# Fetching fewer neighbour rows in a graph kernel: the last tile of each group skips its fetch, and some places are fetched for part of the partitions

## Chip, cores and metric

The kernel runs on one core of a Trainium2 chip, as one launch. The metric is the device time of that launch in microseconds; the median of three runs stands for a kernel. Engines are named as in the profile: PE (matrix products and transposes), DVE (vector), ACT (scalar), POOL (GpSimd), SP (sync).

## The reference, cut to what matters

Sixteen graphs of 1024 nodes have 64 features per node, and a sparse weighted adjacency matrix each. Two residual layers follow each other.

```python
# layer 0
h = maximum(layernorm(x), 0);  x = x + (adj / clip(rowsum(adj), 1)) @ h
# layer 1
h = maximum(layernorm(x), 0)
nb  = neighbours of a node, itself left out
m   = number of neighbours
if m > 10: drop every ceil(m/2)-th neighbour, symmetrically
agg = 0.25*q25 + 0.5*q50 + 0.25*q75     # per channel, interpolated quantiles
                                        # of h over the node and its kept neighbours
x = x + (relu((h + agg) @ W1 + b1) @ W2 + b2) * mask
```

The quantiles need each node's neighbour rows, sorted channel by channel. Most nodes have few neighbours: the adjacency is built so that low node numbers have many and high ones hardly any.

## The kernel before, in words

**Layer 0.** For each graph, pairs of 128-row blocks of the adjacency matrix are loaded by DMAs that ACT issues, turned by PE, copied to SBUF by ACT and multiplied with h. Beside it DVE lists the neighbours of each row (`signs`, `listing`), and `endings` gives each node a place in an order by falling neighbour count. POOL then scatters the node rows to a table `srt` in that order (eight indirect DMAs for one graph), and SP writes the normalized rows to `tab`. A last row of `tab` for each graph holds 1e30 in the channels and -1 behind them: the row of a neighbour that is not there.

**Groups.** Four graphs make a group, and there are four groups. In a group, the sorted nodes are cut into 32 tiles of 128 partitions. Each tile holds 32 successive ranks of each of the four graphs, and a quarter of it (32 partitions) holds 8 successive ranks of each. `CAPS` (line 36) gives the number of neighbours that a tile provides for: 15 for tile 1, then 10, 8, 7, 7, 6 and so on to 1 for tiles 27 to 31. Tile 0, with the nodes of very many neighbours, is handled separately as four long lists. Tiles of one cap form a `Job` (line 875), ten jobs in each group.

**A job.** `Job.run` takes a buffer A (`places`, four of them in turn) with a slot for the node and one for each neighbour. POOL fills one slot of one tile with one indirect DMA of 128 rows (`gather`, line 854): 124 of these for each group. A neighbour that is not there has the index of the 1e30 row. Then `sort` has DVE mark dropped neighbours and run a sorting network with min and max, `weigh` multiplies the sorted places with the weights of the quantiles, and `layers` sums them on PE and runs the two small products. DVE adds the residual to y, and POOL scatters y to the output, one indirect DMA for each tile. A flag (`checked`, line 1397) compares the neighbour counts with the caps; if a count is above its cap, a slow dense path runs in place of these results.

**Order.** DVE and POOL run in the order in which the program writes their instructions. That order is made by `Plan` (line 246), a list scheduler with a clock for each engine and a fixed cost for each operation: an indirect DMA costs 1.27 us on POOL, whatever its width (line 322), a copy on ACT 0.06 us and 0.86 ns for each element. Among the streams ready first, rank decides. The work on ACT, PE and SP is put into order by the tile framework's own scheduler. All engines take their queues strictly in order. The groups 0 to 2 are begun while layer 0 still runs for later graphs; group 3 and the long lists (`lplaces`) come after layer 0.

Of the kernel before, what the change touches and what calls it, by code (L numbers as in the profile page):

```python
# [9 lines left out]
F32 = mybir.dt.float32  # L10
# [8 lines left out]
P = 128  # L19
# [4 lines left out]
HUGE = 1.0e30  # L24
# [11 lines left out]
CAPS = (  # L36
    [0, 15, 10, 8, 7, 7, 6] + [5] * 4 + [4] * 4 + [3] * 6 + [2] * 6 + [1] * 5
)
CAPS2 = [CAPS[1]] + CAPS[2::2]
LONG = (88, 28, 21, 18)  # L40
MAIN = 38
LENT = 20
# [203 lines left out]
class Plan:  # L246
# [25 lines left out]
    def room(self, name, bufs):  # L272

        tiles = self.slots.get(name, ())
        if len(tiles) < bufs:
            return 0.0
        old = tiles[-bufs]
        return INF if self.users[old] else max(self.used.get(old, 0.0), self.ready.get(old, 0.0))

    def at(self, *tiles):  # L280
        return max(self.ready.get(t.tensor.name, INF) for t in tiles)
# [72 lines left out]
def kernel(  # L354
# [27 lines left out]
    with tc.manual_schedule(engines={mybir.EngineType.DVE, mybir.EngineType.Pool}):  # L382
        list_path(tc, x, adj, nodemask, w1, b1, w2, b2, out, go)
# [7 lines left out]
def list_path(ctx, tc, x, adj, nodemask, w1, b1, w2, b2, out, go):  # L391
    nc = tc.nc
    B, N, C = x.shape
# [8 lines left out]
    W = C + 2  # L402
# [4 lines left out]
    RW = R0 + REC  # L407
    NTAU = len(CAPS)
    HP = P // 2
    NF = NG + NG + len(LONG)  # L410

    consts = ctx.enter_context(tc.tile_pool(name="consts", bufs=1))
# [51 lines left out]
    caps4 = consts.tile([P, NTAU], F32, name="caps4")  # L464
    for t, cap in enumerate(CAPS):
        nc.vector.memset(caps4[:, t:t + 1], float(cap if t else N))
    caps2 = consts.tile([P, NTAU // 2], F32, name="caps2")
    for t, cap in enumerate(CAPS2):
        nc.vector.memset(caps2[:, t:t + 1], float(cap))
    nc.vector.memset(caps2[HP:, 0:1], float(N))  # L470

# [33 lines left out]
    turn = consts.tile([P, 1], F32, name="turn")  # L505
    ovf = consts.tile([P, NF], F32, name="ovf")
    nc.vector.memset(ovf, 0.0)
# [5 lines left out]
    tabs = [dram.tile([n * TS, W], F32, name=f"tab{g}") for g, n in enumerate(GROUPS)]  # L513
    whole = dram.tile([B * TS, W], F32, name="whole")
    srt = [dram.tile([GROUPS[g] * N, RW], F32, name=f"srt{g}") for g in range(NG)]
    none = consts.tile([B, W], F32, name="none")
    nc.vector.memset(none[:, :C], HUGE)
    nc.vector.memset(none[:, C:], -1.0)
    for tab, n in zip(tabs, GROUPS):
        nc.sync.dma_start(tab.rearrange("(b t) w -> b t w", t=TS)[:, N, :], none[:n])  # L520
    adj_rows = adj.rearrange("b i j -> (b i) j")
# [4 lines left out]
    plan = Plan(nc)  # L526
    plan.parts.update(tab.tensor.name for tab in tabs)
    nc = plan.nc
# [325 lines left out]
    def gather(dst, src, idx):  # L854
        nc.gpsimd.indirect_dma_start(
            out=dst, out_offset=None, in_=src,
            in_offset=bass.IndirectOffsetOnAxis(ap=idx, axis=0),
        )

    def scatter(dst, src, idx, others):  # L860
        if plan.last is others:
            nc.gpsimd.memset(turn, 0.0)
        ins = nc.gpsimd.indirect_dma_start(
            out=dst, out_offset=bass.IndirectOffsetOnAxis(ap=idx, axis=0),
            in_=src, in_offset=None,
        )

        for other in others:
            tc.declare_no_dep(ins.ins, other, reason="rows of their own")
        others.append(ins.ins)  # L870
        plan.last = others
# [3 lines left out]
    class Job:  # L875
# [1 line left out]


        def __init__(self, pool, n, T, keys, idx, node, mask, nodes_i, table, S, g, name="places",
                     bufs=4, rank=0, half=False, begin=0.0, shared=None, first=0):  # L880
            self.__dict__.update(locals())
            self.short = pool is gat
            self.tag = "" if self.short else "l0" if name == "lplaces0" else "l"
            self.block = BLOCK if self.tag == "l0" else n
            self.bufs1 = 1 if self.tag == "l0" else 2

        def run(self):
            n, T, pool, short = self.n, self.T, self.pool, self.short

            since = []  # L890
            own = () if short else (lambda rank: self.rank,)
            pace = lambda: since[0] + 1.3 * len(since) if not short else 0.0
            yield "POOL", lambda: max(
                self.begin, at(self.idx), room(self.name, self.bufs),
                room("S", 4) if short and not (self.shared and "S" in self.shared) else 0.0,
            ), *own
            A = self.A = new(pool, [P, n, T, W], F32, self.name, self.bufs, users=1)
            lent = LENT if self.tag == "l0" else 0
            order = [*range(lent), *range(n - 1 - MAIN, n - 1)] if lent else range(n - 1)
            progress["ahead"] += T * len(order)  # L900
            parts = self.parts() if self.block < n else None
            if short:
                mine, share = self.S, self.shared
                if share is None:
                    share = {"users": 1, "rows": mine}
                if "S" not in share:
                    S = share["S"] = new(
                        pool, [P, mine_of(share), C], F32, "S", 4, users=share["users"]
                    )
                    nc.sync.dma_start(S, share["rows"][:, :, :C])  # L910
                self.share = share
                self.S = share["S"][:, self.first:self.first + T, :]
            for t in range(T):
                for k in order:
                    if t or k:
                        yield "POOL", pace, *own
                    since.append(since[0] if since else plan.clock["POOL"])
                    plan.own = plan.clock["POOL"]
                    gather(A[:, k + 1, t, :], self.table, self.idx[:, t, k:k + 1])
                    plan.own = None  # L920
                    progress["ahead"] -= 1
                    if k == lent - 1:
                        plan.add(self.moves(parts), self.rank)
                    elif parts and k >= lent and ((k + 2) % self.block == 0 or k == n - 2):
                        plan.add(parts(-(-(k + 2) // self.block) - 1), self.rank)
            if parts:
                yield "DVE", lambda: self.landed if self.left == 0 else INF, self.soon
                yield from self.merge()
                return
            yield "DVE", lambda: max(  # L930
                at(A, self.S) + SLACK,
                *(room(self.tag + name, self.bufs1) for name in ("gone", "wu")),
            ), self.soon
            yield from self.sort()
# [226 lines left out]
        def layers(self, terms, sources):  # L1161
# [63 lines left out]
            for t in range(T):  # L1225
                yield "POOL", lambda: at(y) + LATE
                top = HP if self.half and t == 0 else P
                scatter(out_rows, y[:top, t, :], self.nodes_i[:top, t:t + 1], scatters)
# [70 lines left out]
    def group(g, kept=grp, name=""):  # L1299

        assert GROUPS[g] == 4
        caps, begin, NTAU = CAPS, 1, len(CAPS)
# [76 lines left out]
        dropped = at(table)  # L1379
# [45 lines left out]
        shared = {"users": len(few), "rows": tiles[:, front, :R0]}  # L1425
        for i, ts in enumerate(classes):
            n, T = caps[ts[0]] + 1, len(ts)
            sl = slice(ts[0], ts[-1] + 1)
            job = Job(
                gat, n, T, keys[:, sl, :n - 1], idx[:, sl, :], node[:, sl], mask[:, sl],  # L1430
                nodes_i[:, sl], table, tiles[:, sl, :R0], g,
                half=0 in ts, begin=dropped,
                **(dict(shared=shared, first=ts[0] - few[0][0]) if ts in few else {}),
            )
            plan.add(job.run(), 100 * g + i)
        progress["groups"] = g + 1

    def long_lists(pool):
# [14 lines left out]
        for e, (by, last) in enumerate(((5, 1), (7, 0))):  # L1453
# [4 lines left out]
            )  # L1458
        own_rows = new(pool, [P, len(LONG), RW], F32, "lS", 1)
        for g in range(NG):  # L1460
            lo, num = FIRST[g] * LSUB, GROUPS[g] * LSUB
            nc.sync.dma_start(
                own_rows[lo:lo + num, :, :],
                srt[g][:len(LONG) * num, :].rearrange("(l r) w -> r l w", l=len(LONG)),
            )
        for l in LORDER:
            K = LONG[l]
            n = K + 1
# [110 lines left out]
    for g in range(NG - 1):  # L1579
        plan.add(group(g), -2000)  # L1580
# [9 lines left out]
    with tc.tile_pool(name="long", bufs=1) as pool:  # L1590

        plan.add(group(NG - 1, pool, "last_"), -2000)
        plan.add(long_lists(pool), -1500)
        plan.run()
    nc = tc.nc
# [291 lines left out]
```

## Time and profile before

| | us |
|---|---|
| median of three runs (1734.42 to 1737.37) | 1736.29 |
| the profiled execution | 1737.01 |
| its span | 1735.1 |
| busy: DVE | 1200.8 |
| busy: POOL | 946.9 |
| busy: PE | 781.4 |
| busy: ACT | 557.5 |

The span runs from the first to the last instruction of the profiled execution. A helper records every operation, so nearly all rows carry line 240 (`Timed`); rows are told apart by the tiles that they write and read. On POOL, a row of an indirect DMA is the time on the engine, not the transfer.

### The profile page before, as it was taken

How to read it: one execution, taken by the hardware profiler on the slowest of the kernel's cores; microseconds unless marked ns; L12 is line 12 of the kernel's file. 1: busy time of each engine (PE TensorE's matmuls, PEld its weight loads, DVE VectorE, ACT ScalarE, POOL GpSimd, SP SyncE). 2: the span in 40 equal slices, each digit the busy share in tenths (PEclk: the TensorE clock that was granted, in tenths of full speed). 3: DMA queues.
4: the chain of work that ended last, by engine and by line, in shares of the span. 5: the costliest groups of instructions: out<-in, count | busy, mean ns of one | idle time of the engine just before them, and what ended most of it. 6: DMA issues, size and time to landing. Idle time of an engine off the chain costs nothing. (4 is left out here: it accounts for less than half of the span.)

```text
span 1735.1 us, 14258 instructions
## 1 busy us (share of the span) xinstructions
PE 781.4 (45%) x3203; PEld 483.9 (28%) x3203; DVE 1200.8 (69%) x4061; ACT 557.5 (32%) x1603; POOL 946.9 (55%) x1117
## 2 busy tenths in 40 slices
PE   5877634522686426627644644310200303116576
PEld 3434312321353223314422322200100202114355
DVE  7787954684587356829854655587699536899496
ACT  7766724351373333626533432200000001000011
POOL 0222372575545646554557256576687774658463
PEclk9888866765888666768766866555555556556667
DMA  4454732341154231424523311321211111012000
GB/s 167 149 178 139 205 90 65 108 122 23 45 148 156 64 99 41 140 46 136 150 51 87 93 30 43 72 60 38 50 26 24 25 24 24 19 20 41 15 22 14
DMA packets 133833, 132.30 MB, mean 76 GB/s; under 512 B 99444, under 2 KB 102132, under 8 KB 133620
## 3 DMA queue, kind: packets, MB, share of 16 engines
q10 hardware_dynamic: 34048, 71.31, 12.4%
q0 software_dynamic: 31520, 40.19, 10.6%
q1 hardware_dynamic: 68172, 19.82, 5.3%
q8 instruction: 27, 0.44, 0.1%
q14 instruction: 66, 0.54, 0.1%
HBM read 111.76 MB, written 23.61 MB: 78 GB/s over the span
## 5 line engine op out<-in xcount | busy, mean ns | idle before, releaser
L240 POOL DMA_INDIRECT places<-tab,idx x372 | 367.6, 988 | 121.6 <-issue 110.1
L240 PE MATMUL pt<-ident,prod 128*128 128x128 f32 (+1 forms) x736 | 152.5, 365 | 357.6 <-DVE prod L240 245.8
L240 POOL DMA_INDIRECT srt<-row,to x128 | 131.8, 1030 | 287.1 <-ACT row L240 268.1
L240 PE MATMUL ps_small<-att,h 128*65 128x512 f32 x512 | 266.8, 666 | 33.7 <-issue 19.3
L240 PE MATMUL pt<-ident,at 128*128 128x128 f32 x1024 | 191.6, 339 | 182.3 <-ACT att L240 104.7
L240 PEld LDWEIGHTS pt<-ident,prod 128*128 128x128 f32 (+1 forms) x736 | 123.4, 247 | 388.9 <-issue 211.9
L240 PEld LDWEIGHTS pt<-ident,at 128*128 128x128 f32 x1024 | 149.7, 175 | 239.9 <-ACT att L240 126.1
L240 ACT COPY att<-pt 128x512 f32<-128x512 f32 x256 | 143.3, 582 | 169.9 <-remote 98.3
L240 DVE MAX8 rec<-sg 128x8 f16<-128x256 f16 x512 | 180.1, 414 | 14.3 <-remote 6.4
L240 ACT COPY ot<-pt 128x128 f32<-128x128 f32 (+3 forms) x56 | 22.4, 400 | 476.7 <-remote 194.6
L240 POOL DMA_INDIRECT out_dram<-y,nodes_i x93 | 97.0, 1043 | 121.7 <-DVE y L240 81.4
L240 POOL DMA_INDIRECT places<-tab,last_idx x124 | 132.8, 1071 | 52.0 <-issue 37.1
L240 POOL DMA_INDIRECT lplaces<-whole,lidx x125 | 138.5, 1108 | 38.1 <-issue 37.2
L240 ACT ACTIVATE sg<-at 128x1024 f16<-128x1024 f32 x128 | 134.6, 1053 | 52.4 <-DVE rec L240 15.7
L240 PEld LDWEIGHTS ps_small<-att,h 128*65 128x65 f32 x512 | 77.2, 157 | 165.0 <-issue 144.4
L240 PE MATMUL ps_small<-ot,w_sb 128*128 128x128 f32 (+3 forms) x112 | 55.9, 591 | 127.8 <-ACT ot L240 80.9
L240 DVE TENSOR_TENSOR sg<-sg,keyed 128x1024 f16<-128x1024 f16 x128 | 87.3, 682 | 18.0 <-ACT sg L240 14.7
L240 DVE TENSOR_TENSOR places<-places,other 128x128 f32<-128x128 f32 (+6 forms) x160 | 56.4, 355 | 25.9 <-remote 12.4
L240 ACT ACTIVATE wu<-wu 128x39 f32<-128x39 f32 (+9 forms) x40 | 9.4, 234 | 191.8 <-DVE wu L240 166.2
L240 PE MATMUL ps_small<-w_sb,hid 128*128 128x64 f32 x256 | 53.2, 350 | 29.3 <-issue 21.6
L240 ACT ACTIVATE hid<-ps_small,b_sb 128x128 f32<-128x128 f32 (+2 forms) x56 | 28.1, 502 | 111.7 <-remote 72.9
L240 PEld LDWEIGHTS ps_small<-ot,w_sb 128*128 128x128 f32 (+1 forms) x112 | 23.2, 254 | 141.7 <-ACT ot L240 87.8
(289 smaller groups left out, 1621.3 us busy)
## 6 DMA issues: line engine op xcount, KB each, us to landing
at<-in_adj_dram ACTq DMA_DIRECT2D x64, 1024.0 KB
places<-tab,idx POOLq DMA_INDIRECT x372
whole<-tab SPq DMA_DIRECT2D x4, 1057.0 KB
tab<-row SPq DMA_DIRECT2D x16, 264.0 KB
xt<-in_x_dram ACTq DMA_DIRECT2D x16, 256.0 KB
S<-srt SPq DMA_DIRECT2D x12, 192.0 KB
y<-srt SPq DMA_DIRECT2D x12, 192.0 KB
srt<-row,to POOLq DMA_INDIRECT x128
```

Source lines behind the costliest of these rows:

```text
L240: ins = getattr(self._engine, op)(*args, **kwargs)
```

## The change

A table `QUARTERS` gives nine of the tiles a cap for each quarter. In each group tile 31 then gets no fetch at all, and eight places (three of tile 1 and one each of tiles 2, 5, 10, 20 and 26) are fetched for 32, 64 or 96 partitions only. The partitions that are left out get the row of a missing neighbour by ScalarE copies from a constant tile `void`, 32 partitions by 66 elements each. They are written in `run` ahead of the job's fetches. The comparison with the caps in `checked` uses the quarters' caps.

```diff
+QUARTERS = {
+    1: (15, 13, 12, 12), 2: (10, 10, 10, 9), 5: (7, 7, 6, 6), 10: (5, 5, 4, 4), 14: (4, 4, 4, 4),
+    20: (3, 3, 2, 2), 26: (2, 2, 1, 1), 30: (1, 1, 1, 1), 31: (0, 0, 0, 0)}
+def quarters(t):
+    return QUARTERS.get(t, (CAPS[t],) * 4)
...
+    for t in QUARTERS:
+        for q, cap in enumerate(quarters(t)):
+            nc.vector.memset(caps4[q * QUART:(q + 1) * QUART, t:t + 1], float(cap))
...
-    none = consts.tile([B, W], F32, name="none")
-    nc.vector.memset(none[:, :C], HUGE)
-    nc.vector.memset(none[:, C:], -1.0)
+    void = consts.tile([P, W], F32, name="void")
+    nc.vector.memset(void[:, :C], HUGE)
+    nc.vector.memset(void[:, C:], -1.0)
+    none = void[:B, :]
...
+            if short:
+                for t in range(T):
+                    for k in order:
+                        top = QUART * sum(cap > k for cap in quarters(self.tiles[t]))
+                        for low in range(top, P, QUART):
+                            nc.scalar.copy(
+                                A[low:low + QUART, k + 1, t, :], void[low:low + QUART, :]
+                            )
             for t in range(T):
                 for k in order:
...
-                    plan.own = plan.clock["POOL"]
-                    gather(A[:, k + 1, t, :], self.table, self.idx[:, t, k:k + 1])
-                    plan.own = None
+                    top = P
+                    if short:
+                        top = QUART * sum(cap > k for cap in quarters(self.tiles[t]))
+                    if top:
+                        plan.own = plan.clock["POOL"]
+                        gather(A[:top, k + 1, t, :], self.table, self.idx[:top, t, k:k + 1])
+                        plan.own = None
```

For each group this makes 123 fetches of 124, eight of them narrower (two of 32 partitions, five of 64, one of 96), and 21 copies on ACT. Over the kernel, that is 492 fetches in place of 496, 32 of them narrower, and 84 copies.

More of the change, by code (lines that the diff above doesn't have):

```diff
@@ L409, in list_path @@
     HP = P // 2
+    QUART = P // 4
     NF = NG + NG + len(LONG)
@@ L879, in __init__ @@
         def __init__(self, pool, n, T, keys, idx, node, mask, nodes_i, table, S, g, name="places",
-                     bufs=4, rank=0, half=False, begin=0.0, shared=None, first=0):
+                     bufs=4, rank=0, half=False, begin=0.0, shared=None, first=0,
+                     tiles_of=None):
             self.__dict__.update(locals())
             self.short = pool is gat
+            self.tiles = tiles_of
             self.tag = "" if self.short else "l0" if name == "lplaces0" else "l"
@@ L1431, in group @@
                 nodes_i[:, sl], table, tiles[:, sl, :R0], g,
-                half=0 in ts, begin=dropped,
+                half=0 in ts, tiles_of=ts, begin=dropped,
                 **(dict(shared=shared, first=ts[0] - few[0][0]) if ts in few else {}),
```

## The prediction

> **What bounds the kernel now.** I read the busy times and their rows by slice first, then the waits of POOL, the stretches of the span, and last the order of time at the end.
>
> ```profile
> PE 781.4 (45%) x3203; PEld 483.9 (28%) x3203; DVE 1200.8 (69%) x4061; ACT 557.5 (32%) x1603; POOL 946.9 (55%) x1117
> ...
> DVE  7787954684587356829854655587699536899496
> ACT  7766724351373333626533432200000001000011
> POOL 0222372575545646554557256576687774658463
> ...
> L240 POOL DMA_INDIRECT places<-tab,idx x372 | 367.6, 988 | 121.6 <-issue 110.1
> ```
>
> No engine is full. A fetch costs POOL 988 ns plus 0.30 us to the next one, so 1.25 to 1.29 us, and 0.7 busy on POOL is really about 0.9 occupied. The kernel has two stages. In the first (to about 1115 us, where the last node rows are scattered) layer 0 runs with the jobs of groups 0 to 2 between it. Here POOL waits for the others, as its waits of the first 1000 us show (total, times, longest):
>
> ```profile
> POOL srt L240 <- ACT row L240: 247.2, 25, 61.0
> POOL places L240 <- issue: 86.6, 284, 0.3
> POOL out_dram L240 <- DVE y L240: 71.5, 7, 13.7
> ```
>
> 247.2 us of waiting for finished node rows: a POOL that is done earlier only waits longer there. What holds this stage up are chains between ACT, PE and DVE, with DVE standing still up to 24 us at a time:
>
> ```profile
> 767.50 0.32 DVE L240 TENSOR_SCALAR ln_v<-ln_v 128x8 f32<-128x8 f32 x1 [23.98 <-remote]
> ```
>
> The second stage has the rest of group 2, the long lists and group 3. By stretches of 100 us (busy PE, PEld, DVE, ACT, POOL):
>
> ```profile
> 1300.00:1400.00 100.00, 16.48 (x56) 10.93 (x56) 76.37 (x234) 3.92 (x10) 78.05 (x73) 0.53 0.14 24
> 1400.00:1500.00 100.00, 16.19 (x82) 12.71 (x82) 64.03 (x196) 6.90 (x19) 60.77 (x73) 0.55 0.11 23
> 1500.00:1600.00 100.00, 39.25 (x167) 30.96 (x167) 92.19 (x279) 6.36 (x22) 67.20 (x65) 0.59 0.16 29
> ```
>
> Up to 1400 POOL feeds without a break (78 busy and 73 gaps of 0.3 make 100). From 1500 on DVE is the full one. POOL's order of time at the end shows who waits for whom:
>
> ```profile
> 1627.60 0.94 POOL L240 DMA_INDIRECT places<-tab,last_idx  x1 [0.30 <-issue]
> 1648.82 2.25 POOL L240 DMA_INDIRECT out_dram<-y,lnodes_i  x1 [20.27 <-DVE lother L240]
> ...
> 1673.68 1.29 POOL L240 DMA_INDIRECT places<-tab,last_idx  x1 [0.30 <-issue]
> ...
> 1719.41 0.96 POOL L240 DMA_INDIRECT out_dram<-y,last_nodes_i  x1 [13.54 <-DVE y L240]
> ...
> 1729.52 0.96 POOL L240 DMA_INDIRECT out_dram<-y,lnodes_i  x1 [0.19 <-POOLq L385]
> ```
>
> POOL stands 20 us behind a long list on DVE, makes the last fetch at 1673.7, waits for y, and ends the kernel with nine scatters. So a microsecond saved on POOL is worth nothing in the first stage, something between 1115 and 1500, and little after that.
>
> **The change part by part.**
>
> *Four fetches removed.* 4 x 1.25 = 5.0 us of POOL. In the built order, tile 31 of groups 0 and 1 lies in the first stage: 2.5 us that POOL then waits longer for rows. Value 0 (2.5 if that cover is gone). Groups 2 and 3 lie in the second: 2.5 us less feeding.
>
> *32 fetches narrowed.* No row shows an indirect DMA of fewer than 128 partitions. These rows, all 128 wide, carry 8, 656 and 4096 bytes for each partition:
>
> ```profile
> L240 POOL DMA_INDIRECT tab<-drop,didx x8 | 7.8, 976 | 31.2 <-DVE didx L240 15.1 <-DVE gfound L240 11.8 <-DVE keys L240 2.8
> L240 POOL DMA_INDIRECT srt<-row,to x128 | 131.8, 1030 | 287.1 <-ACT row L240 268.1 <-issue 17.6 <-ACT h L240 0.2
> L240 POOL DMA_INDIRECT gat_rows<-in_adj_dram,hnodes_i x4 | 3.9, 968 | 40.6 <-PE pt L240 22.1 <-DVE base L240 11.7 <-DMA y<-srt 6.6
> ```
>
> Bytes do not matter; the row could be all fixed cost, or all a cost for each of 128 descriptors. The Trainium skill's page "DMA: Bandwidth & Descriptors" (section "Anatomy of one DMA — SWDGE (gpsimd) path") calls descriptor generation small, with many descriptors to be had before the cost shows: by it a narrow fetch saves nothing, which speaks against this part. The page "Perfetto Trace Analysis" (section "DMA Instruction — SWDGE (GPSIMD)") says that the profiler's end on such a row is the end of descriptor generation: by it the 0.95 us could shrink with the width. Proportionally, a group saves 5 x 0.48 + 2 x 0.71 + 0.24 = 4.1 us, so 16 us in all; of the ten narrowed fetches in the second stage (two of group 2, eight of group 3) 4.1 + 2 x 0.48 = 5.0 us can count. A fetch that became slower by being narrow has no reason in any row. I take 0, the rows being flat, and keep -5 for the range.
>
> *84 copies added on ACT.* The nearest row is the 64-wide copy of the same kind:
>
> ```profile
> L240 ACT COPY prod<-S 128x64 f32<-128x64 f32 x16 | 3.8, 239 | 0.0
> ```
>
> 84 x 0.24 = 20 us of ACT, about 15 of them (63 copies) in groups 0 to 2, most in the first stage, where ACT is 27 to 75% busy and on the chain that makes the rows. In the second stage ACT is under 12% busy and they are free. Each copy also waits until its buffer is free, that is for the last DVE or fetch signal of the job four before; behind it in ACT's queue stand the copies of turned blocks, the sign passes, the row normalizations and ACT's own loads of `at` and `xt`. DVE, PE and POOL's row scatters wait for those. In the built order nine job fillings of groups 0 to 2 carry a wait for a DVE signal, typically some two DVE signals after the one that ACT has just waited for: about 1 us each if DVE is the late one. Bounds: 0, and 15 + 9 = 24 us. ACT's next item mostly waits for a later DVE signal still, so I take a fifth of the 15: +3 us.
>
> *Constants.* 36 memsets more on DVE at the start. The 32 old ones take 0.64 us, so 0.7 more, ahead of a wait of 2.76 us for `mrow`:
>
> ```profile
> 4.25 0.32 DVE L466 MEMSET caps<- 128x1 f32 x22
> ...
> 8.53 0.23 DVE L491 CAST gat_rows<-mrow 128x128 f32<-128x128 uint8 x1 [2.76 <-DMA mrow<-in_nodemask_dram]
> ```
>
> Value 0; 0.7 if that load came sooner.
>
> *What is moved.* The planner's clocks differ, so the order on POOL changes from about the middle of layer 0 on. DVE's work is the same apart from the constants. Between the last row scatter and the last fetch POOL now has 334 indirect DMAs in place of 348: two fetches removed, four of group 2 moved ahead into the first stage, and eight output scatters moved behind the last fetch (29 DMAs follow it, not 21). For POOL alone 14 x 1.26 = 18 us sooner. DVE decides how much counts: from the last graph's class step (`hot`) to the end, it has 1534 instructions, not 1549; 15 at the 0.30 us that DVE's average one takes from 1100 on (484 us busy, 1594 instructions) are 4 us. DVE's listed waits from 1400 to 1500 are 35 us, part of them for fetches; I let 3 us go there. The moved scatters wait for y now, beside the 13.54 us wait: covered. If it is gone they cost their 8 x 1.27 = 10 us. The row of scatters after the last wait could be six long in the new order, not nine; but the second long list's y comes only at 1726.8 on DVE, so of 1729.5 at most 2.4 us can go, and I take 1. SP issues one table write (`tab<-row`) later past loads of S; group fetches wait for the table only at a group's end, so 0. The other moves in the first stage I cannot price singly: 0, with one DVE stall of 24 us more or less as both ends.
>
> *Sum:* -2.5 (inside the 18 us, so covered by DVE, 0) - 4 - 3 - 0 + 3 - 1 (the end) = -5. Against the profiled execution, 1737.0 - 5 = 1732.0. That execution is 0.7 us above the median of 1736.3, so 1731.3; I say 1731. What a measurement here tells from no change is 0.2%, or 3.5 us.
>
> **The rivals.**
>
> *Hidden.* The saved fetches and the moved work sit where DVE or rows are late anyway, and the copies eat the rest: -5 + 5 = 0, 1733 to 1740. For it: 247 us of POOL waiting, and 92% DVE. Against: DVE's own work in the second stage falls.
>
> *Slower: ACT held up by its fillings.* The place is ACT's queue between 350 and 1100 us, its price up to 24 us. It decides once over 8.5 us (5 + 3.5) comes onto the row chain, 0.13 us for each of the 63 copies, about half of the time of one. For it: ACT shows waits of 9 to 27 us there, so its lateness is already felt. Against: ACT is idle for half of that stage. With 10 to 20 us net: 1746 to 1756.
>
> *The new order costs or saves a stall in layer 0.* One of the 24 us: 1755, or 1707 to 1712 with one less.
>
> *The change does not do what it says* when a count is above a quarter's cap: then the dense path would run and the time be several times as long. The neighbour counts of these inputs stay within every quarter's cap, so I give it nothing.
>
> **How the numbers follow.** Forecast (1719 to 1732, narrow fetches at either bound) 0.42; a stall less 0.06; hidden 0.19; ACT held up 0.23; a stall more 0.10. Faster by over 3.5 us: 0.42 + 0.06 = 0.48, less 0.01 for the edge, 0.47. Slower: 0.23 + 0.10 + 0.03 of the hidden case, 0.36. Within: 0.17. The range leaves out the stall less and part of the two slow cases: 1714 to 1753. The forecast's own range is 1719 to 1732.
>
> **What would show it.** POOL's row of fetches at 64 or 32 partitions: near 950 ns, my value, or near 480 and 240. ACT's copies from `void` at some 0.24 us, and idle time ahead of them with a DVE releaser: few us in all, against tens if ACT is held up. The last row scatter near 1115 us: later by over 8 us means layer 0 paid, and I am wrong. The last fetch before 1674 by several us with DVE over 90% busy after it: my second stage. If the last fetch comes early and the end does not, the gain was hidden.

## The result, and the profile after

The changed kernel takes 1785.39 us (median of four runs, 1774.2 to 1793.7), the kernel before, measured beside it, 1735.36 us: 1.029 times as long, 95% interval 1.023 to 1.035. The forecast was 1731 us with a range up to 1753; it was wrong in sign. The profiled execution took 1785.97 us, its span is 1784.2 us. In each comparison below the ratio is to runs of the kernel before that were made beside it, because that kernel itself took 1735 to 1759 us in five of the comparisons and 1395 to 1397 us in two; runs more than 1.5% above the fastest of their kernel are left out of the ratios.

The page of the changed kernel, the rows that answer to those of before:

```profile
PE 774.8 (43%) x3203; PEld 485.0 (27%) x3203; DVE 1201.0 (67%) x4097; ACT 578.8 (32%) x1687; POOL 923.7 (52%) x1115
...
DVE  8877935676584683677616483775689429798496
ACT  7767715442462454454317141200000001000010
POOL 0222372575436645635752636676277754576443
...
L247 POOL DMA_INDIRECT places<-tab,idx x369 | 362.5, 982 | 145.5 <-issue 109.4
```

DVE's busy time is the same (1201.0 against 1200.8 us) and POOL's is 23 us less (13 of them in rows of fetches to `places`; most of the rest are other rows that came out shorter at the same count). So the 49 us of span are idle time of DVE, which no busy time shows. POOL's waits of the first 1000 us:

```profile
POOL srt L247 <- ACT row L247: 229.5, 26, 59.8
POOL places L247 <- issue: 84.7, 278, 0.3
POOL out_dram L247 <- DVE y L247: 49.6, 5, 14.0
```

These three are 41 us smaller than before (one new wait, of 25.2 us for `prod`, eats part of that), and yet layer 0 ends later: the last row scatter starts at 1132.0 us, not 1114.8 (kernel before, then changed; the times at the end of each row are the first and last start):

```profile
L240 POOL DMA_INDIRECT srt<-row,to x128: 957/963/2247, 63.2 to 1114.8; - x128
L247 POOL DMA_INDIRECT srt<-row,to x128: 956/960/2237, 62.0 to 1132.0; - x128
```

The stretches of the second stage (busy PE, PEld, DVE, ACT, POOL), one of the kernel before and four of the changed kernel:

```profile
1200.00:1300.00 100.00, 12.55 (x36) 7.73 (x36) 82.37 (x286) 1.67 (x3) 72.28 (x69) 0.50 0.18 37
...
1200.00:1300.00 100.00, 26.69 (x86) 17.25 (x86) 61.09 (x233) 6.34 (x18) 49.76 (x49) 0.51 0.16 37
1300.00:1400.00 100.00, 2.69 (x14) 1.97 (x13) 91.23 (x264) 1.37 (x4) 78.66 (x75) 0.52 0.14 25
1400.00:1500.00 100.00, 10.62 (x52) 9.21 (x53) 47.34 (x146) 5.64 (x16) 51.93 (x63) 0.53 0.10 20
1500.00:1600.00 100.00, 21.52 (x89) 17.63 (x89) 86.89 (x283) 8.10 (x28) 65.18 (x70) 0.55 0.11 21
```

DVE has 61 us of work between 1200 and 1300, where it had 82 before. Of its 39 idle us there, 29 are one wait, which the order of time shows:

```profile
1235.26 7.47 PE L247 MATMUL pt<-ident,prod 128*128 128x128 f32 x24 [28.77 <-DVE prod L247]
...
1253.14 0.94 POOL L247 DMA_INDIRECT lplaces<-whole,lidx  x1 [0.30 <-issue]
...
1258.51 0.58 ACT L247 COPY ot<-pt 128x512 f32<-128x512 f32 x1 [22.67 <-remote]
...
1264.31 0.86 DVE L247 SCALAR_TENSOR_TENSOR y<-ps_small,recs,y 128x64 f32<-128x64 f32 x4 [29.11 <-PE ps_small L247]
```

DVE has finished `prod` at 1235.2 and next in its queue is the addition to y of the same job, which needs the whole chain PE, ACT, PE, ACT, PE. In the built order of the changed kernel this addition stands directly behind its own `prod`; in the trace of the kernel before no addition to y that follows a `prod` has to wait. And the chain is slow: PE ends its 24 products at 1242.7, but ACT gets the signal at 1258.5, 15.8 us later and 4.4 us after POOL's string of fetches ends.

At the end of the kernel POOL waits in pieces, first in the kernel before (the third of its waits, 13.54 us, stands in the prediction), then in the changed one:

```profile
1685.17 0.97 POOL L240 DMA_INDIRECT out_dram<-y,last_nodes_i  x1 [8.42 <-DVE y L240]
...
1697.96 0.96 POOL L240 DMA_INDIRECT out_dram<-y,last_nodes_i  x1 [7.64 <-DVE y L240]
```

```profile
1700.60 1.00 POOL L247 DMA_INDIRECT out_dram<-y,lnodes_i  x1 [24.74 <-DVE lrem L247]
1701.90 1.69 POOL L247 DMA_INDIRECT places<-tab,last_idx  x1 [0.30 <-issue]
...
1726.14 0.95 POOL L247 DMA_INDIRECT out_dram<-y,lnodes_i  x1 [9.78 <-DVE y L247]
...
1734.79 0.96 POOL L247 DMA_INDIRECT out_dram<-y,last_nodes_i  x1 [7.58 <-DVE y L247]
...
1750.18 1.09 POOL L247 DMA_INDIRECT out_dram<-y,last_nodes_i  x1 [10.44 <-DVE lother L247]
...
1769.63 0.96 POOL L247 DMA_INDIRECT out_dram<-y,lnodes_i  x1 [9.18 <-DVE y L247]
```

The last fetch comes at 1701.9 (before 1673.7), and from its start to the end of the span it is 82 us, not 61. Of the 49 us, 17 are there when layer 0 ends, 28 at the last fetch, the rest behind it. Behind the last fetch the waits for y are 30 us before (three) and 37 now (four); the eight scatters that were moved there make up most of the other 14.

The rows of the parts that the prediction priced came as it priced them. The rows of the narrow fetches of tile 1 (by their place in the order 64, 32 and 32 partitions) and the row of the copies:

```profile
229.07 0.92 POOL L247 DMA_INDIRECT places<-tab,idx  x1 [0.30 <-issue]
230.29 0.89 POOL L247 DMA_INDIRECT places<-tab,idx  x1 [0.30 <-issue]
231.49 0.87 POOL L247 DMA_INDIRECT places<-tab,idx  x1 [0.31 <-issue]
```

```profile
L247 ACT COPY places<-void 32x66 f32<-32x66 f32 x84 | 20.4, 243 | 67.6 <-DVE prod L247 35.2 <-DVE other L247 29.1 <-issue 2.2
```

A quarter of the partitions costs 0.88 us where all cost 0.94 (the median). A copy takes 0.24 us, but ACT stood idle for 67.6 us ahead of the copies. So two theories were left: the copies hold up ACT's queue, or the replanned order costs the time.

### The profile page after: what moved, and what is told of

The parts are those of the page before. It is cut to its first block, busy times and chain, and to the rows that moved or that the text cites. A ratio compares the mean times of both kernels' runs of the same rounds, so it can differ in the third digit from the quotient of the medians.

```text
span 1784.2 us, 14442 instructions
## 1 busy us (share of the span) xinstructions
PE 774.8 (43%) x3203; PEld 485.0 (27%) x3203; DVE 1201.0 (67%) x4097; ACT 578.8 (32%) x1687; POOL 923.7 (52%) x1115
## 4 chain that ended last, share of the span: by engine, by line
DVE 39%; another core or an unknown queue 20%; issue 13%; POOL 9%; PE 9%; ACT 7%; DMA 3%; DVEq 0%; ACTq 0%; SPq 0%; POOLq 0%
DVE places L247 7%; PE ps_small L247 5%; DVE rec L247 4%; DVE other L247 4%; POOL lplaces L247 4%; PE pt L247 4%; DVE lplaces L247 3%; POOL places L247 3%; DVE sg L247 2%; DVE l0other L247 2%; ACT sg L247 2%; DVE lother L247 1%; DVE lfound L247 1%; DVE prod L247 1%
## 5 line engine op out<-in xcount | busy, mean ns | idle before, releaser
L247 POOL DMA_INDIRECT places<-tab,idx x369 | 362.5, 982 | 145.5 <-issue 109.4
L247 POOL DMA_INDIRECT lplaces<-whole,lidx x125 | 131.8, 1054 | 38.1 <-issue 37.5
L247 POOL DMA_INDIRECT places<-tab,last_idx x123 | 124.8, 1015 | 37.5 <-issue 36.6
L247 DVE TENSOR_TENSOR places<-other,places 128x128 f32<-128x128 f32 (+5 forms) x136 | 48.8, 366 | 17.2 <-remote 6.9
```

Source lines behind the costliest of these rows:

```text
L247: ins = getattr(self._engine, op)(*args, **kwargs)
```

## Experiments: the work or the order

One kernel does the old work in the new order, another the new work in the old order. The planner is told of work that isn't there, or not told of work that is (`real` is the engine without the planner's clock). This holds the order of DVE and POOL; ACT's, made by the framework, differs at 133 of its 1603 other rows from the changed kernel's in o1_order, and at 115 from that of the kernel before in o2_work. The edits, shortened:

```diff
 # o1_order: the copies are only counted, every fetch is full
-    nc.scalar.copy(A[low:low + QUART, k + 1, t, :], void[low:low + QUART, :])
+    plan.note("ACT", "copy", (A[low:low + QUART, k + 1, t, :], void[low:low + QUART, :]), {})
-    gather(A[:top, k + 1, t, :], self.table, self.idx[:top, t, k:k + 1])
+    gather(A[:, k + 1, t, :], self.table, self.idx[:, t, k:k + 1])   # tile 31: fetched, not counted
 # o2_work: the copies are made, not counted; tile 31 is counted, not fetched
-    nc.scalar.copy(...)
+    real.scalar.copy(...)
 # o3_pool: as o2_work, the copies on POOL
+    real.gpsimd.tensor_copy(...)
```

> All fetches at full width, as in the kernel before (496 of them), and no copies from void; but DVE and POOL run in the order of the changed kernel, because the planner still counts the copies and the missing fetches. Theory 'order' (the replanned order costs the time): about 1785 us, as the changed kernel, ratio 1.02 to 1.03. Theory 'copies' (84 copies wait in ACT's queue and hold what stands behind them): 1731 to 1741 us, ratio 1.00. Half and half would be near 1760.

> The changed kernel's work (492 fetches, 32 of them narrow, 84 copies on ACT), but DVE and POOL run in the order of the kernel before, because the planner does not see the copies and counts the missing fetches as if they were there. Theory 'copies': 1760 to 1785 us, ratio 1.015 to 1.03, with some 60 us of idle time ahead of ACT's copies. Theory 'order': 1731 to 1741 us, ratio 1.00, even if ACT waits ahead of the copies.

> As the kernel with the old order and the changed work, but the 84 copies run on POOL ahead of each job's fetches, so that ACT has none. Theory 'copies': the loss goes, 1731 to 1745 us (POOL pays the copies itself, at 0.1 to 0.3 us each 8 to 25 us, mostly in its own waiting). Theory 'order': 1731 to 1745 us too. If it is above 1755, the fills cost wherever they run, because the jobs of a group then start on a buffer that is freed late.

Measured: o1_order 1.032 (1.020 to 1.044), o2_work 1.0043 (1.0012 to 1.0073), o3_pool 0.9575 (0.946 to 0.969). The order costs the time, without a single copy or narrow fetch. The work costs 0.4%, or 7.5 us of 1751, although ACT's idle time ahead of the copies was even longer there:

```profile
L932 ACT COPY places<-void 32x66 f32<-32x66 f32 x84 | 20.4, 243 | 151.7 <-DVE prod L247 112.4 <-DVE other L247 25.9 <-remote 8.0
```

The long wait before y is there in o1_order too, as long as in the changed kernel, behind a signal of PE that again comes 16.3 us after its products end (1259.1 to 1275.4):

```profile
1251.62 7.46 PE L247 MATMUL pt<-ident,prod 128*128 128x128 f32 x24 [27.76 <-DVE prod L247]
...
1275.42 0.59 ACT L247 COPY ot<-pt 128x512 f32<-128x512 f32 x1 [48.76 <-remote]
...
1281.22 0.86 DVE L247 SCALAR_TENSOR_TENSOR y<-ps_small,recs,y 128x64 f32<-128x64 f32 x4 [29.66 <-PE ps_small L247]
```

The third result was not foreseen by any theory: the same fills on POOL make the kernel 4.3% faster than before.

To see which idle time differs, DVE's idle times over 0.25 us are sorted here by the engine whose signal the instruction behind each waits for (worked out from the traces, us; "none" where no wait is recorded):

```
kernel                              span   own DVE    PE   ACT   DMA   none
before                              1735       215   125    99    24     13
changed                             1784       214   175    95    32      6
o1_order (old work, new order)      1790       230   175    91    23      8
o2_work (new work, old order)       1753       204   132   117    25     13
```

In both traces of the new order DVE waits 50 us more for PE than in that of the kernel before. (A later trace of the changed kernel, a1_after, has 231 us for PE and 176 for its own: the amounts move from trace to trace, the direction does not.) And there is a second thing: DVE loses 204 to 230 us waiting for its own signals. A signal is called late here when it arrives well after the instruction that sends it has ended. The trace of the kernel before shows such signals directly:

```profile
255.84 0.70 PE L240 MATMUL ps_small<-ident,msg 65*128 65x65 f32 x4 [21.85 <-issue]
...
266.41 0.59 ACT L240 COPY att<-pt 128x512 f32<-128x512 f32 x1 [9.57 <-remote]
...
273.87 0.94 POOL L240 DMA_INDIRECT places<-tab,idx  x1 [0.30 <-issue]
...
277.61 0.59 ACT L240 COPY att<-pt 128x512 f32<-128x512 f32 x1 [10.61 <-remote]
...
281.15 0.16 DVE L240 TENSOR_SCALAR deg<-ps_small 128x4 f32<-128x4 f32 x1 [24.68 <-remote]
```

PE's products that DVE needs here end at 256.5, and the signal arrives at 281.1. "remote" in these rows is a late signal of PE. In the whole trace, 63 signals of PE (by up to 26.2 us), 130 of DVE (by up to 8.3) and 16 of ACT arrive when no instruction of their engine has ended in the 0.8 us before; all of them after 200 us, and POOL's first fetch is at 212. The count misses those behind which something newer had ended, as at 281.1. The row that the prediction showed at 767.50 is partly of this kind: its "remote" is a signal of ACT that arrives 4.5 us after ACT's last instruction.

## Experiments: what lets the late signals through

First theory: a string of fetches without any other instruction on POOL holds them back. Row scatters have a 0.12 us memset between them, and few late signals beside them.

```diff
     def gather(dst, src, idx):
+        real.gpsimd.memset(turn, 0.0)        # brk1: each fetch; brk4: each fourth
         nc.gpsimd.indirect_dma_start(
```

> The kernel before with a POOL memset of 128x1 ahead of each of its 621 fetches (as stands between row scatters already); the order on all engines is unchanged. In the traces PE's and DVE's signals come up to 25 us late, mostly while POOL strings fetches together (late time of PE's signals 0.55 us for each us of fetching, against 0.11 for each us of the row scatters, which have a memset between them). Theory 'late signals' (the string of fetches without a break delays them): the stalls go, 1600 to 1700 us, ratio below 0.98. Theory 'order only' (the stalls are waits of the program's own order): POOL loses 0.02 to 0.1 us for each fetch, 1736 to 1760 us, ratio 1.00 to 1.015.

> The changed kernel with the same memset ahead of each fetch. Theory 'late signals': the loss of the change goes with the stalls, within 10 us of the kernel before with the memsets, 1600 to 1700 us. Theory 'order only': it stays some 45 us above it, 1785 to 1810 us.

> The kernel before with the memset ahead of every fourth fetch only. Theory 'late signals': part of the gain, 1640 to 1725 us, if a break every 5 us lets the signals through. Theory 'order only': 1734 to 1745 us.

> The changed kernel with the memset ahead of every fourth fetch only. Theory 'late signals': 1640 to 1740 us and within 15 us of the kernel before with the same memsets. Theory 'order only': 1780 to 1795 us.

Measured, in this order: 1.0039 (1.0011 to 1.0067), 1.036 (1.028 to 1.044), 1.0033 (1.0005 to 1.006) and 1.032 (1.023 to 1.041). The theory fell: the memsets change nothing, and the two orders stay 3% apart.

Second theory, from the trace of o3_pool: there POOL stands still for the landing of fetches before a fill, and two late signals of PE arrive just behind it (at 238.99 and 239.05):

```profile
236.27 0.88 POOL L247 DMA_INDIRECT places<-tab,idx  x1 [0.30 <-issue]
238.59 0.24 POOL L932 COPY places<-void 32x66 f32<-32x66 f32 x1 [1.45 <-DMA places<-tab,idx]
239.27 0.98 POOL L247 DMA_INDIRECT places<-tab,idx  x1 [0.44 <-issue]
```

So the kernels before and after got real pauses, in an unchanged order. Beside them two kernels were planned with another constant, for a third and fourth order:

```diff
+        if count >= 16 and last.tensor.name == dst.tensor.name:      # t5, t6
+            real.gpsimd.tensor_copy(rest[:last.shape[0]], last[:, :1])
+            count = 0
```

```diff
-LATE = 14.0
+LATE = 20.0                                                          # p1, p2
```

> The kernel before with a pause of POOL after every sixteenth fetch of a job: a copy of one column of the place just fetched to a scratch tile, so that POOL waits for that fetch's landing (38 pauses of about 1.5 to 2 us). The order on ACT, PE and DVE is unchanged. The kernel with the fills on POOL was 4.25% faster than the kernel before, and at 237 us three late signals of PE came through right behind a wait of POOL for landings. Theory 'pauses let signals through': ratio 0.95 to 0.98. Rival 'the fills on POOL helped otherwise' (a shift of this one order): POOL loses up to 38 x 2 = 76 us, mostly in its own waiting, ratio 1.00 to 1.02.

> The changed kernel with the same pauses. Theory 'pauses': 3 to 5% below the changed kernel, so ratio 0.98 to 1.00 to the kernel before. Rival: ratio 1.03 to 1.05.

> The kernel before, planned with 20 us in place of 14 us between the end of the PE chain and the DVE addition to y, and between y and its scatter (the constant LATE). The work is the same; 1947 of 8673 DVE instructions stand elsewhere. If the time follows the order (which instruction meets a late signal), it moves by 1 to 3% either way; if the replanning of the change did harm only through the clock of ACT's copies, it stays within 1%.

> The changed kernel, planned with 20 us in place of 14 us. Theory 'order' (DVE stands 29 us before y at 1264 us because y was placed right behind the products that it waits for): the stall goes and 20 to 45 us come back, ratio 1.00 to 1.015. Theory that the missing fetches and copies cost in themselves: ratio stays 1.02 to 1.03.

Measured: t5_before_pause16 0.954 (0.949 to 0.960), t6_after_pause16 0.983 (0.973 to 0.993). 39 pauses, for which POOL stands idle 70 us in all, give 4.6% to the kernel before and about as much to the changed one (0.983 where it was 1.029 without them). The rows of the 31 on `places`:

```profile
L859 POOL COPY rest<-places x31: 178/183/731, 236.5 to 1615.8; 128x1 f32<-128x1 f32 x31
...
  DMA places<-tab,idx: 43.9, 23
```

(The row has minimum, median and maximum in ns; below it, POOL's idle time before these copies and how often.) DVE's waits for its own signals fall from 215 to 141 us, those for PE from 125 to 107. The 24 us wait at 281 is gone. t5_before_pause16 beats both kernels in this condition. But the orders are still 3.0% apart (0.983 to 0.954): in t6 the wait before y is still 25 us. That the pauses work by letting signals through is shown for the kernel before alone: there the late time, summed over the signals counted above, falls from 598 to 446 us for PE and from 241 to 141 for DVE. In the changed kernel it hardly falls (668 to 646, 205 to 203), where DVE waits 176 us in place of 214 for its own signals and 163 in place of 175 for PE; why it gains as much stays open.

p1_before_late20 took 1.017 (1.0125 to 1.022), p2_after_late20 1.041 (1.036 to 1.046). My expectation for p2 was a miss: another plan did not bring the time back. DVE then waited 249 us for PE, at other places.

## Experiments: is the order bad in itself?

> The kernel before with a pause of POOL after every eighth fetch (77 pauses, a wait for the landing of the fetch just issued, 1.9 us at the median where they came after every sixteenth). Theory 'pauses let late signals through': DVE's waits for its own and for PE's signals fall further, ratio 0.93 to 0.955. If POOL is by then the bound, the 38 further pauses (70 us of POOL) come back as waits for landings: ratio 0.955 to 0.975.

> The changed kernel with the same 77 pauses. With a pause after every sixteenth fetch the changed kernel stood 3.0% above the kernel before with the same pauses (0.983 to 0.954). Theory 'the order costs by the late signals that it meets': the difference shrinks to below 1.5%. Theory 'the order costs by itself' (DVE would wait for PE even if PE's signals were prompt): it stays at 2.5 to 3.5%.

> The kernel before with sixteen POOL memsets of 128x1 in a row (16 x 0.12 = 1.9 us) after every sixteenth fetch, in place of the wait for a landing; same places as the pauses that gave 0.954. If any break of 1.9 us in the issue of fetches lets the signals through: ratio 0.945 to 0.965. If POOL must stand still (or wait for landings) for it: ratio 1.00 to 1.02.

> The changed kernel's work, with a planner that sees the copies but counts the four missing fetches at 1.27 us each, as if they were there. 823 of 8673 DVE instructions stand elsewhere than in the kernel before, and 1177 elsewhere than in the changed kernel. Theory 'the order of the changed kernel is a bad one, made by the four missing fetches': ratio 0.99 to 1.015. Theory 'any replanning here costs, since the kernel before has a chosen order': ratio 1.02 to 1.04.

```diff
-        if count >= 16 and last.tensor.name == dst.tensor.name:
+        if count >= 8 and last.tensor.name == dst.tensor.name:       # t7, t8
```

```diff
-            real.gpsimd.tensor_copy(rest[:last.shape[0]], last[:, :1])
+            for _ in range(16):                                      # t9
+                real.gpsimd.memset(turn, 0.0)
```

```diff
+                    else:      # q2, q3: tile 31 counted by the planner, not fetched
+                        plan.note("POOL", "indirect_dma_start", ...)
```

Here the kernel before took 1394.8 us, the other condition. In these traces one signal of PE and one of DVE are late by the count above (0.8 and 0.9 us), not 63 and 130. So there was nothing for pauses to let through, and they only cost: t7 1.115 (1.112 to 1.118), t8 1.125 (1.122 to 1.127) and t9 1.064 (1.061 to 1.067). Whether sixteen memsets would do in place of a wait stays open. q2_seen_copies took 1.017 (1.015 to 1.020). The pair t7 and t8 tells something all the same: with equal pauses and prompt signals the orders are 0.7% apart (1568.3 to 1557.6 us).

> The changed kernel itself, once more. In the last four runs the kernel before took 1395 us on their chip, not 1735 to 1760 us as on the others, and the traces there show hardly a late signal (2 to 3 for each engine, against 80 to 130). Theory 'the new order costs by the late signals that it meets': on a chip where the kernel before takes 1395 us the ratio is 0.99 to 1.01; on one where it takes 1735 to 1760 us it is 1.02 to 1.035. Theory 'the order costs by itself': 1.02 to 1.035 on either.

> The changed work with a planner that sees the copies but counts the four missing fetches as if they were there, once more. On the chip where the kernel before takes 1395 us its ratio was 1.017. On a chip where it takes 1735 to 1760 us: 0.99 to 1.015 if the missing fetches in the planner made the bad order, 1.02 to 1.04 if any replanning costs there.

> The changed kernel itself, a third time, for the chance of a chip with prompt signals. Theory 'the new order costs by the late signals that it meets': 0.99 to 1.01 where the kernel before takes 1395 us, 1.02 to 1.035 where it takes 1735 to 1760 us. Theory 'the order costs by itself': 1.02 to 1.035 on either.

a1_after and q3_seen_copies met late signals. The two runs of the changed kernel that count took 1788.2 and 1795.5 us beside 1754.1, about 1.02 (its other two took 1826 and 1833), and q3_seen_copies 1.019 (1.0145 to 1.024). So it is not shown that counting the missing fetches as if they were made takes away any of the loss: a planner that sees only 84 copies of 0.12 us also makes an order that is 2% worse. That order costs 1.7% with prompt signals too (q2_seen_copies), so it is bad by itself.

a2_after met prompt signals: 1406.5 us beside 1397.3, ratio 1.0072 (1.0056 to 1.0089). Its page, and the same chain and y:

```profile
PE 741.5 (53%) x3203; PEld 465.7 (33%) x3203; DVE 1201.8 (86%) x4097; ACT 578.8 (41%) x1687; POOL 942.7 (67%) x1115
```

```profile
959.62 7.46 PE L247 MATMUL pt<-ident,prod 128*128 128x128 f32 x24 [28.46 <-DVE prod L247]
...
965.38 0.94 POOL L247 DMA_INDIRECT lplaces<-whole,lidx  x1 [0.30 <-issue]
...
966.62 0.94 POOL L247 DMA_INDIRECT lplaces<-whole,lidx  x1 [0.30 <-issue]
...
967.12 0.59 ACT L247 COPY ot<-pt 128x512 f32<-128x512 f32 x1 [6.56 <-PE pt L247]
...
972.91 0.86 DVE L247 SCALAR_TENSOR_TENSOR y<-ps_small,recs,y 128x64 f32<-128x64 f32 x4 [13.35 <-PE ps_small L247]
```

With nearly the same busy times on every engine the same program ends 380 us sooner. The wait before y is 13.35 us: that is the bad place in the order, with a prompt chain. The other 15.8 us of the 29.11 are the late signal. The sorted idle times of DVE are 0 for its own signals, 36 for PE, 21 for ACT and 81 us for DMAs. And here POOL's fetches run on without a break from 940 to 975, through the signal that ACT gets within 0.1 us of the end of the products: a string of fetches alone does not make signals late.

So for the order of the changed kernel both are needed: it makes DVE wait more for PE's signals, which costs 0.7% (9 us) with prompt signals and 2 to 3% (35 to 55 us) where each of them can be 10 to 25 us late.

## Why the prediction was wrong, point by point

- *Fetches removed and narrowed: 0.* Right as far as is shown: no run has these fetches alone, and together with the copies they cost 0.4%. The narrow rows are 0.87 to 0.89 us at 32 partitions and 0.92 at 64; the reading that the fixed cost rules was right, and a row that shrinks in proportion to the width, as I drew from the Trainium skill's page "Perfetto Trace Analysis" (section "DMA Instruction — SWDGE (GPSIMD)"), is ruled out here.
- *84 copies on ACT: +3.* Somewhat small. New work in the old order costs 7.5 us (2 to 13), the constants and the saved fetches included; the bounds of 0 and 24 hold it. The rival "ACT held up by its fillings", with 0.23, is not what happened: ACT's idle time before the copies grew from 67.6 to 151.7 us in o2_work, at a cost of 0.4% in all. It was idle time that hardly anybody waited for.
- *What is moved: -7 (4 + 3), in the second stage.* This is the step that failed, with its sign: I let the new order gain 8 us (4 + 3 here, 1 at the end, nothing in the first stage), and old work in the new order costs 3.2%, 56 us (35 to 77). I counted how many instructions lie between two marks and multiplied by their mean duration. That says nothing of waits. The order could be read before the run: one addition to y stood directly behind its own `prod`, and the trace of before showed what DVE's waits for a signal of PE can cost, up to 24.7 us and "remote". I took "fewer instructions after the mark" for a gain and let 3 us of waits go.
- *First stage: 0, one stall more or less.* The last row scatter came 17 us late, which the prediction named as its mark of being wrong. The rival "the new order costs a stall" (0.10, 1755 us) had the mechanism; its size of one stall was too small, since the second stage paid too, and its chance far too low. Not all of the 17 us need be the order: the last scatter starts at 1148.3 in o1_order, but at 1128.7 in o2_work too, beside runs of the kernel before that were themselves 16 us longer. A replanned order was taken for a coin that falls either way. All the orders that were run with late signals are slower than that of the kernel before: 1.017, 1.019, 1.029 and 1.041.
- *The end: -1.* It cost 21 us. The moved scatters were not covered: there was no single wait for y to hide them behind, neither before (8.4, 7.6 and 13.5 us) nor after (9.8, 7.6, 10.4 and 9.2). The prediction's own fall-back of 10 us for them comes nearer.

## What to carry to other kernels

When a change passes through a planner, price the order as well as the work: run the old work in the new order, or read from the built order which instruction stands directly behind the chain that it waits for, and put the price of a wait from the trace on it. Idle time before an instruction ("67.6 us ahead of the copies") is no cost until one sees who waits behind it. And where idle times with no visible releaser add up to hundreds of us, look for late signals first: in that condition 39 small waits on POOL gave more here than the change to the work, and in the other condition such waits only cost.

## What was not expected of the hardware

- In the traces of 1680 to 1830 us, signals of PE arrive up to 25 us and more after the instruction ended, signals of DVE, to itself too, up to 8 or 9 us. Of the 49 PE signals in the trace of before that are over 3 us late, 30 arrive while POOL stands idle, 1.7 to 5.0 us behind its last instruction, and 19 while it issues fetches. A 0.12 us memset between fetches does not let them through, and with prompt signals the same fetches do no harm. Why they are late no run shows.
- In two comparisons of seven the signals were prompt, and the unchanged kernel took 1395 to 1397 us in place of 1735 to 1759. The pauses gain 4.6% in the one condition; twice as many cost 11.5% in the other. What makes the condition was not found: runs numbered with the same chip (11) met both. The late traces also hold fewer signal records, 2063 for DVE's 2677 signalling instructions in the changed kernel against 2677 in a2_after. Every run on record was recorded with a span and a clock, so whether the recording itself has a part in the lateness is untested. A version that is better in both conditions was not found either.
- An indirect DMA of 32 partitions holds POOL for 0.87 to 0.89 us, one of 128 for 0.94 at the median.
